# Single-row LSTM as a 2x2 Strassen product, with new tile counts and a planner that reserves result tiles

## The chip, the cores and the metric

The kernel runs on one core of one Trainium2 chip. The metric is device time in microseconds (us), from runs of the whole kernel. The engines are TensorE (PE, matrix products), VectorE (DVE), ScalarE (ACT), GpSimd (POOL) and SyncE (SP, whose queue issues nearly all the DMAs). PEld is the part of TensorE that loads a stationary 128x128 tile.

## The reference

Four layers work on x of 128 batches, 64 rows, 256 features, in float32. Each layer is `x = layernorm(x + f(x))`.

- Layer 0: three graph convolutions with widths 512, 1024 and 256.
- Layer 1: projection on the eigenvectors of a graph Laplacian, two dense layers, and back.
- Layer 2: two graph convolutions with a ReLU give h, and then LSTMs are run over windows of p rows of h, for p = 1, 2, 3, 4 in turn; the last hidden state of each window replaces the last row of that window.
- Layer 3: attention over the 64 rows, masked by the graph.

The part that the change touches is the LSTM with p = 1, where every window is a single row, so that there is no recurrence:

```python
g = x_t @ Wih.T + h @ Whh.T + bias            # h = 0
i, f, gg, o = jnp.split(g, 4, axis=-1)
c = sigmoid(f) * c + sigmoid(i) * tanh(gg)    # c = 0
h = sigmoid(o) * tanh(c)
```

With p = 1 only the gates i, g and o are needed: 768 of the 1024 columns of the weights.

## The kernel before, in words

The 8192 rows are 64 tiles of 128 rows; a *group* is four tiles (8 batches, 512 rows). Layer 0 runs first for all 16 groups, with the eigenvectors worked out beside it; then SBUF is handed over to a second phase, which takes layers 1, 2 and 3 of a group in one go. This second phase is what the change touches.

**Units.** A *unit* is two groups (the last four groups are units of one). A unit notes operations in the order layer1, to_lstm and the LSTMs of p = 1, 2, 3 for each of its groups, then p = 4 for the two together (function `four`), then from_lstm and layer3 for each. Three units are under way at a time (`UNITS`), so one near its end, one in its middle and one at its start can fill each other's waits.

**The planner.** No operation of the second phase is issued where it is written. `Plan.note` records it with an estimated cost, what must come before it and the tiles it touches. `Plan.run` then goes through the recorded operations with a simple clock: for each engine it takes those that could start within 0.02 us of the earliest one, and among these the one with the smallest `rank` (the group number, so the oldest group first). What comes out is a fixed order of instructions for each engine. A tile gets a slot when the first operation that touches it is planned; an operation is ready only when a slot is free (`t = max(t, min(s))`, line 178). Units younger than the oldest leave a few slots of each kind to it (`MOST`).

**Tiles.** PSUM has eight slots of one bank (`ps`). In SBUF there are six work tiles of 128x1024 (`w`; each group's h, called hT, lives in one from to_lstm to from_lstm), four half-size work tiles (`v`), six gate tiles (`gates`), four cell tiles (`c`), four of hidden states (`hs`) and three attention tiles (`att`).

**LSTM with p = 1** (`lstm`, called twice at lines 1290 and 1291, 32 windows of 8 batches each, n = 256). For each half h of the hidden features and each gate of i, g, o it runs two products of 128x128 by 128x256 into one PSUM tile, and ScalarE takes the result straight to a gate tile with bias and tanh (the sigmoid is written with a tanh, which is why factors 0.5 and `op0=ALU.add` with 1.0 appear). VectorE then does one `scalar_tensor_tensor` for i and g, ScalarE a tanh, and VectorE a `scalar_tensor_tensor` that writes h back into hT. For a group this is 24 products of 256 columns.

**Halves** (`halves`, line 1439). The second step of p = 2 and the steps of p = 4 of paired groups already use a seven-product scheme: sums of the weights (`add_weights`) and of the moving operands are built on VectorE, seven products take the place of eight, and VectorE puts the results together with additions that read PSUM.

**The weights.** The four `wih` and three `whh` tiles of 1 MB are loaded by SP at the handover (`load`, lines 857 and 1144), in the order wih0, wih1, whh1, wih2, whh2, wih3, whh3. wih0 is that of p = 1. They are laid out as (k p) f -> p k f, with k the half of the 256 input features.

All the operations of the second phase are issued from one line, 156 (`emit`), so that the profile is read by tile names: `ps<-w,wih` is a product of a work tile with wih, `gates<-gates,ps` an addition of a PSUM tile into a gate tile, and so on.

## Time and profile before

| what | value |
|---|---|
| median of 3 runs | 2471.87 us (2471.45 to 2472.79) |
| time of the profiled execution | 2474.36 us |
| span of the profiled execution | 2472.6 us |
| PE busy | 2438.2 us (99%), 15500 products |
| DVE busy | 1618.9 us (65%), 5676 instructions |
| ACT busy | 1072.3 us (43%), 2610 instructions |
| granted TensorE clock | 0.996 |
| from 861 us to 2472 us (second phase): PE, DVE, ACT busy | 1583.25, 962.74, 757.48 us of 1611 |

How to read the lines: a line of a group is "line engine operation out<-in shape xcount | busy us, mean ns of one | idle time of the engine before them and what ended it". A line of the window view gives for a stretch of the span the length, then the busy time of PE, PEld, DVE, ACT and POOL, each with its number of instructions, then the clock, the DMA share and GB/s. Durations of instructions that follow each other closely overlap, so mean times count is more than busy time. One float32 product of the program appears as two MATMUL instructions.

### The profile page before, as it was taken

How to read it: one execution, taken by the hardware profiler on the slowest of the kernel's cores; microseconds unless marked ns; L12 is line 12 of the kernel's file. 1: busy time of each engine (PE TensorE's matmuls, PEld its weight loads, DVE VectorE, ACT ScalarE, POOL GpSimd, SP SyncE). 2: the span in 40 equal slices, each digit the busy share in tenths (PEclk: the TensorE clock that was granted, in tenths of full speed). 3: DMA queues.
4: the chain of work that ended last, by engine and by line, in shares of the span. 5: the costliest groups of instructions: out<-in, count | busy, mean ns of one | idle time of the engine just before them, and what ended most of it. 6: DMA issues, size and time to landing. Idle time of an engine off the chain costs nothing.

```text
span 2472.6 us, 40811 instructions
## 1 busy us (share of the span) xinstructions
PE 2438.2 (99%) x15500; PEld 2162.5 (87%) x15500; DVE 1618.9 (65%) x5676; ACT 1072.3 (43%) x2610; POOL 137.4 (6%) x316
## 2 busy tenths in 40 slices
PE   9999999999999999999999999999999999999997
PEld 7788888878887899989978999999998997988996
DVE  6888787778887274583674476476458468374336
ACT  2343343333333354444434444444444444445555
POOL 0000000000000010010010000000001001010002
PEclk9999999999999999999999999999999999999999
DMA  6000000000000110010000001001001000000000
GB/s 225 9 1 18 10 9 10 9 10 9 10 1 1 64 56 1 1 35 1 1 18 18 1 1 35 1 1 35 1 1 35 1 1 18 1 10 1 1 1 27
DMA packets 27973, 42.69 MB, mean 17 GB/s; under 512 B 2945, under 2 KB 22145, under 8 KB 27777
## 3 DMA queue, kind: packets, MB, share of 16 engines
q1 hardware_dynamic: 27424, 39.81, 4.6%
q8 instruction: 122, 2.00, 0.3%
q14 instruction: 75, 0.61, 0.1%
q10 hardware_dynamic: 352, 0.28, 0.0%
HBM read 26.45 MB, written 13.63 MB: 16 GB/s over the span
## 4 chain that ended last, share of the span: by engine, by line
PE 93%; DVE 5%; POOL 1%; DMA 1%; ACT 0%; issue 0%; SPq 0%; ACTq 0%; POOLq 0%; DVEq 0%
PE ps L156 61%; PE ps L940 31%; DVE X L156 1%; DVE D L52 1%; DVE st L156 1%; PE pc L296 1%; DMA XA<-in_x_dram 1%; DVE gates L156 0%; POOL rs L156 0%; DVE tw L52 0%; DVE w L156 0%; ACT gates L156 0%; DVE h L52 0%; DVE u L52 0%; DVE mv L156 0%
## 5 line engine op out<-in xcount | busy, mean ns | idle before, releaser
L156 PE MATMUL ps<-w,wih 128*128 128x168 f32 (+2 forms) x4144 | 753.7, 315 | 0.9 <-DVE gates L156 0.9
L156 PEld LDWEIGHTS ps<-w,wih 128*128 128x128 f32 x4144 | 647.6, 191 | 38.1 <-issue 6.9
L156 ACT ACTIVATE gates<-ps,cbi 128x168 f32<-128x168 f32 (+2 forms) x832 | 342.8, 418 | 368.5 <-PE ps L156 360.3
L156 PE MATMUL ps<-hs,whh 128*128 128x168 f32 (+1 forms) x1952 | 344.8, 291 | 0.0
L156 PEld LDWEIGHTS ps<-hs,whh 128*128 128x128 f32 x1952 | 289.2, 191 | 1.7 <-issue 1.4
L156 PE MATMUL ps<-w,sums 128*128 128x128 f32 x1776 | 237.1, 275 | 0.0
L156 DVE SCALAR_TENSOR_TENSOR gates<-gates 128x256 f32<-128x256 f32 (+2 forms) x220 | 84.0, 382 | 222.8 <-ACT gates L156 222.2
L940 PE MATMUL ps<-aw,h 128*128 128x256 f32 x1024 | 227.2, 379 | 0.0
L156 PEld LDWEIGHTS ps<-w,sums 128*128 128x128 f32 x1776 | 217.5, 192 | 0.6 <-issue 0.5
L940 PEld LDWEIGHTS ps<-aw,h 128*128 128x128 f32 x1024 | 192.9, 190 | 25.9 <-ACT h L949 0.5
L156 ACT ACTIVATE gates<-gates,cbi 128x256 f32<-128x256 f32 x272 | 116.4, 497 | 206.6 <-DVE gates L156 206.5
L949 ACT ACTIVATE h<-h 128x512 f32<-128x512 f32 x128 | 80.5, 630 | 196.6 <-DVE h L52 196.5
L156 DVE TENSOR_TENSOR gates<-gates,ps 128x256 f32<-128x256 f32 x340 | 128.7, 417 | 21.3 <-PE ps L156 15.9
L940 PE MATMUL ps<-ss,tw 128*128 128x256 f32 x512 | 117.9, 380 | 0.0
L940 PE MATMUL ps<-ss,aw 128*128 128x256 f32 x512 | 117.3, 379 | 0.0
L940 PE MATMUL ps<-m,aw 128*128 128x256 f32 x512 | 117.1, 380 | 0.0
L156 DVE SCALAR_TENSOR_TENSOR c<-gates,c 128x256 f32<-128x256 f32 (+2 forms) x156 | 57.2, 367 | 88.6 <-ACT gates L156 88.2
L940 PE MATMUL ps<-aw,m 128*128 128x512 f32 x256 | 114.8, 594 | 0.1
L940 PEld LDWEIGHTS ps<-ss,aw 128*128 128x128 f32 x512 | 96.6, 190 | 12.8
L940 PEld LDWEIGHTS ps<-ss,tw 128*128 128x128 f32 x512 | 96.3, 190 | 12.9 <-issue 0.2
L156 DVE TENSOR_TENSOR gates<-v,ps 128x256 f32<-128x256 f32 x136 | 55.5, 417 | 79.5 <-ACT v L156 47.7
L940 PEld LDWEIGHTS ps<-m,aw 128*128 128x128 f32 x512 | 95.6, 190 | 12.6 <-issue 0.5
(314 smaller groups left out, 3743.0 us busy)
## 6 DMA issues: line engine op xcount, KB each, us to landing
out_dram<-X SPq DMA_DIRECT2D x64, 128.0 KB, 1.7
rest<-XA SPq DMA_DIRECT2D x10, 512.0 KB, 2.6
X<-rest SPq DMA_DIRECT2D x10, 512.0 KB, 3.2
XA<-in_x_dram SPq DMA_DIRECT2D x18, 256.0 KB, 6.2
wih<-in_c_ih_dram SPq DMA_DIRECT2D x4, 1024.0 KB, 7.4
aw<-in_a_w_dram SPq DMA_DIRECT2D x3, 1024.0 KB, 10.8
X<-in_x_dram SPq DMA_DIRECT2D x12, 256.0 KB, 5.9
whh<-in_c_hh_dram SPq DMA_DIRECT2D x3, 1024.0 KB, 9.3
```

The costliest lines, as they stand in the source:

```text
L52: return getattr(self.engine, name)(out, *args, **kw)
L156: getattr(e, name)(*[real(x) for x in args], **{k: real(v) for k, v in kw.items()})
L296: PE.matmul(out, lhsT, rhs, start=True, stop=True)
L940: PE.matmul(out, lhsT, rhs, start=start, stop=stop)
L949: S.activation(dst, src, AF.Relu)
```

## The change: what it does

Seven things change together.

1. The two calls of `lstm` with p = 1 are replaced by one call of a new function `single`. It splits the 768 gate columns in two halves m of three 128-column tiles r, the 256 input features in two halves, and the 512 columns of hT in two halves of 32 windows, and works out the 2x2 block product by seven products instead of eight, for each r: 21 products of 128x128 by 128x256 for a group. Sums of the moving operand (T1 to T4) and of the results are made by VectorE.
2. `add_single` makes the weight sums for it once (three new 128x384 tiles, and a fourth that overwrites a block of wih0).
3. wih0 is loaded without the f columns and in a new order, by eight DMAs instead of one.
4. A product now also claims the tiles of SBUF that its result will go to (`also`): it is planned only when a gate tile, and in `halves` and `single` the half-size work tile, is free. Gate tiles that belong together (two, or three in `single`) are claimed together (`tiles`, `along`).
5. Slots: work tiles 6 to 7, gates 6 to 5, att 3 to 2, c 4 to 3.
6. The rank of operations of all engines but PE is the group number plus a third of the time from which the operation is ready. PE keeps the old rank.
7. `unit` calls `add_single` before the other weight sums.

```diff
@@ -92,6 +92,8 @@
         self.tag, self.shape, self.real, self.slot = tag, list(shape), real, None
         self.left, self.until, self.past = 0, 0.0, []
+        self.along = []
     def part(self):
         free = self.shape[1:]
         return Part(self, np.arange(int(np.prod(free))).reshape(free), (0, self.shape[0]), [])
@@ -121,12 +123,23 @@
     def tile(self, tag, shape, real=None):
         return Tile(tag, shape, real).part()
-    def note(self, engine, calls, cost, ready=0.0):
+    def tiles(self, n, tag, shape):
+        parts = [self.tile(tag, shape) for _ in range(n)]
+        for x in parts:
+            x.tile.along = [y.tile for y in parts if y is not x]
+        return parts
+    def note(self, engine, calls, cost, ready=0.0, also=()):
         op = Op()
         op.unit = self.unit
         op.engine, op.calls, op.cost, op.group, op.rank = engine, calls, cost, self.group, len(self.ops)
         op.before, op.after, op.tiles, op.ready, op.start = set(), [], [], ready, None
+        for x in also:
+            op.tiles.append(x.tile)
+            x.tile.left += 1
         for name, args, kw in () if callable(calls) else calls:
             for i, x in enumerate(list(args) + list(kw.values())):
                 if not isinstance(x, Part):
@@ -163,7 +176,9 @@
         def rank(op):
             if op.engine == "PE" and not todo and len(left) <= LASTS:
                 return -left[op.group]
-            return op.group or 99
+            if op.engine == "PE":
+                return op.group or 99
+            return (op.group or 99) + op.ready / 3
         def candidates(guard):
             oldest = min([u for u in going if u] or [0])
@@ -175,7 +190,7 @@
                     for tile in op.tiles:
                         if tile.real is None and tile.slot is None:
                             s = self.slots[tile.tag]
-                            t = max(t, min(s))
+                            t = max(t, sorted(s)[len(tile.along)])
                             if (guard and op.unit != oldest and
                                     sum(x < 1e9 for x in s) <= self.MOST.get(tile.tag, 1) - held.get((oldest, tile.tag), 0)):
@@ -201,7 +216,7 @@
                         able[op.engine].append(op)
             t, op = (candidates(True) if todo or len(left) > LASTS else None) or candidates(False)
             e = op.engine
-            for tile in op.tiles:
+            for tile in [x for tile in op.tiles for x in [tile] + tile.along]:
                 if tile.real is None:
                     s = self.slots[tile.tag]
                     tile.slot, tile.unit = s.index(min(s)), op.unit
@@ -739,10 +754,10 @@
 EPS = 1e-5
 UNITS = 3
 ENDING = (14, 15)
-WIDE = 6
-GATES = 6
-ATT = 3
-CELLS = 4
+WIDE = 7
+GATES = 5
+ATT = 2
+CELLS = 3
 OUTS = 4
 LASTS = 3
 SINGLE = 4
@@ -1141,7 +1156,16 @@
     psb = ctx.enter_context(tc.tile_pool(name="psb", bufs=1, space=bass.MemoryType.PSUM, reuse_waits="tile"))
     wih, whh = [], []
     for i in range(4):
-        wih.append(load(wb, f"wih{i}", c_ih[i], "(k p) f -> p k f", [P, 2, 1024], p=P))
+        if i:
+            wih.append(load(wb, f"wih{i}", c_ih[i], "(k p) f -> p k f", [P, 2, 1024], p=P))
+        else:
+            wih.append(wb.tile([P, 2, 2, 3, P], F32, name="wih0"))
+            w = c_ih[0].rearrange("(k p) f -> p k f", p=P)
+            for m, r, n, f in ((0, 0, 2, 0), (1, 0, 2, 512), (0, 2, 1, 768), (1, 2, 1, 896)):
+                for k in range(2):
+                    nc.sync.dma_start(wih[0][:, k, m, r:r + n, :].rearrange("p r n -> p (r n)"), w[:, k, f:f + n * P])
         whh.append(load(wb, f"whh{i}", c_hh[i], "(k p) f -> p k f", [P, 2, 1024], p=P) if i else None)
     att = []
     for i in range(ATT):
@@ -1189,15 +1213,26 @@
             V.tensor_sub(S3, a11, a21, ready=ready)
             ways[p].append([a11, a12, a22, S1, S2, S3, S4])
-    def products(calls):
+    def add_single():
+        s = plan.tile("sums", [P, 3, 3, P], wb.tile([P, 3, 3, P], F32, name="sums1"))
+        w = plan.tile("sums", [P, 2, 2, 3, P], wih[0])
+        a11, a12, a21, a22 = (w[:, k, m] for m in range(2) for k in range(2))
+        V.tensor_add(s[:, 0], a21, a22, ready=12.0)
+        V.tensor_sub(s[:, 1], s[:, 0], a11, ready=12.0)
+        V.tensor_sub(s[:, 2], a12, s[:, 1], ready=12.0)
+        V.tensor_sub(a21, a11, a21, ready=12.0)
+        ways[1] = [a11, a12, a22, s[:, 0], s[:, 1], a21, s[:, 2]]
+    def products(calls, also=()):
         size = lambda x: x.at.size if isinstance(x, Part) else int(np.prod(x.shape[1:]))
         cost = sum(max(0.001673 * size(c[2]) + 0.003, 0.223) for c in calls)
-        plan.note("PE", [("matmul", (o, l, r), {"start": a, "stop": z}) for o, l, r, a, z in calls], cost)
-
-    def run(out, pairs, first=True, last=True):
+        plan.note("PE", [("matmul", (o, l, r), {"start": a, "stop": z}) for o, l, r, a, z in calls], cost, also=also)
+    def run(out, pairs, first=True, last=True, also=()):
         n = len(pairs)
-        products([(out, l, r, first and i == 0, last and i == n - 1) for i, (l, r) in enumerate(pairs)])
+        products([(out, l, r, first and i == 0, last and i == n - 1) for i, (l, r) in enumerate(pairs)], also)
     def turns(pairs):
         plan.note("PE", [("transpose", (out, in_, ident), {}) for out, in_ in pairs], 0.109 * len(pairs))
@@ -1287,7 +1322,8 @@
             V.scalar_tensor_tensor(as3(h, 4), rs_row.unsqueeze(1).to_broadcast([P, 4, P]), cb1[:, c:c + 1], p,
                                    op0=ALU.mult, op1=ALU.add, cost=0.666)
             S.activation(hT[:, c, :, :].rearrange("p n b -> p b n"), as3(h, 8), AF.Relu, scale=2.0, cost=0.933)
-        for p, first, nw in ((1, 0, 32), (1, 32, 32), (2, 0, 32), (3, 0, 21)):
+        single(hT)
+        for p, first, nw in ((2, 0, 32), (3, 0, 21)):
             lstm(hT, p, first, nw)
         return hT
@@ -1393,8 +1429,8 @@
                        lambda h, w: hT[:, h, 32 * w + 1:32 * w + 32:2, :])
                 return
             gate = []
-            for h in range(2):
-                G = plan.tile("gates", [P, 1024])[:, :len(names) * n].rearrange("p (q n) -> p q n", n=n)
+            for G in plan.tiles(2, "gates", [P, 1024]):
+                G = G[:, :len(names) * n].rearrange("p (q n) -> p q n", n=n)
                 gate.append({q: G[:, i] for i, q in enumerate(names)})
             if p > 1 and not t and not only:
                 c = plan.tile("c", [P, 512])[:, :2 * n].rearrange("p (h n) -> p h n", h=2)
@@ -1409,10 +1445,10 @@
                     outs = [(wh[:, k, m], hs[:, k, :]) for k in range(2)] if t else []
                     if t and h == 0 and q in names[:2]:
-                        run(pp, ins, last=False)
+                        run(pp, ins, last=False, also=[gate[h][q]])
                         run(pp, outs, first=False)
                     else:
-                        run(pp, ins + outs)
+                        run(pp, ins + outs, also=[gate[h][q]])
                     S.activation(gate[h][q], pp, AF.Tanh, bias=bias[:, j:j + 1], scale=0.5 if q == "g" else 0.25)
                     if q == "g":
                         to = gate[h]["g"] if t or p == 1 else c[:, h, :]
@@ -1442,7 +1478,7 @@
         bias = cbi[:, p - 1, :]
-        G = [plan.tile("gates", [P, 1024]).rearrange("p (w m q n) -> p w m q n", w=2, m=2, q=2) for _ in range(2)]
+        G = [x.rearrange("p (w m q n) -> p w m q n", w=2, m=2, q=2) for x in plan.tiles(2, "gates", [P, 1024])]
         both = work().rearrange("p (s i n) -> p s i n", s=2, i=4)
         def eights(v):
@@ -1466,7 +1502,7 @@
                 bank = ps4((P, 2, 2, P))
                 for at, i in enumerate(which):
                     for q in range(2):
-                        run(bank[:, at, q, :], [(ways[p][s][weight[i]][:, q, h, :], moving[i][s]) for s in range(2)])
+                        run(bank[:, at, q, :], [(ways[p][s][weight[i]][:, q, h, :], moving[i][s]) for s in range(2)], also=[a, u1])
                 return bank[:, 0], bank[:, 1]
             p1, p2 = two(0, 1)
@@ -1499,6 +1535,53 @@
                     V.scalar_tensor_tensor(rows(h, w), eights(G[h][:, w, 1, 1, :]), 1.0, eights(G[h][:, w, 0, 0, :]),
                                            op0=ALU.add, op1=ALU.mult)
+    def single(hT):
+        bias = cbi[:, 0, :]
+        x = [[hT[:, k, 32 * w:32 * w + 32, :] for w in range(2)] for k in range(2)]
+        T = work().rearrange("p (i n) -> p i n", i=4)
+        T1, T2, T3, T4 = (T[:, i].rearrange("p (w b) -> p w b", b=8) for i in range(4))
+        V.tensor_sub(T1, x[0][1], x[0][0])
+        V.tensor_sub(T2, x[1][1], T1)
+        V.tensor_sub(T3, x[1][1], x[0][1])
+        V.tensor_sub(T4, x[1][0], T2)
+        moving = (x[0][0], x[1][0], x[1][1], T4, T1, T2, T3)
+        weight = (0, 1, 6, 2, 3, 4, 5)
+        G = [x.rearrange("p (w m n) -> p w m n", w=2, m=2) for x in plan.tiles(3, "gates", [P, 1024])]
+        for r in range(3):
+            u1 = work2()[:, :256]
+            a, b, c12, d = (G[r][:, w, m] for w in range(2) for m in range(2))
+            def two(*which):
+                bank = ps4((P, 2, 256))
+                for at, i in enumerate(which):
+                    run(bank[:, at], [(ways[1][weight[i]][:, r, :], moving[i])], also=[a, u1])
+                return bank[:, 0], bank[:, 1]
+            p1, p2 = two(0, 1)
+            S.copy(u1, p1)
+            V.tensor_add(a, u1, p2)
+            p6, p7 = two(5, 6)
+            V.tensor_add(c12, u1, p6)
+            V.tensor_add(b, c12, p7)
+            p5, p3 = two(4, 2)
+            V.tensor_add(d, b, p5)
+            V.tensor_add(c12, c12, p5)
+            V.tensor_add(c12, c12, p3)
+            p4, _ = two(3)
+            V.tensor_add(b, b, p4)
+            for m, name in ((0, "io"[r // 2]), (1, "go"[r // 2])):
+                j = 2 * "ifgo".index(name) + (r if r < 2 else m)
+                S.activation(G[r][:, :, m, :], G[r][:, :, m, :], AF.Tanh, bias=bias[:, j:j + 1],
+                             scale=0.5 if name == "g" else 0.25)
+            if r < 2:
+                i, g = G[r][:, :, 0, :], G[r][:, :, 1, :]
+                V.scalar_tensor_tensor(g, i, 1.0, g, op0=ALU.add, op1=ALU.mult)
+                S.activation(i, g, AF.Tanh, scale=0.5)
+        for h in range(2):
+            V.scalar_tensor_tensor(hT[:, h, :, :].rearrange("p (w a) b -> p w (a b)", w=2), G[2][:, :, h, :], 1.0,
+                                   G[h][:, :, 0, :], op0=ALU.add, op1=ALU.mult)
     def four(hTs):
         n = 128
@@ -1518,6 +1601,7 @@
     def unit(groups):
         if groups[0] == 0:
+            add_single()
             add_weights(2, 30.0)
             add_weights(4, 60.0)
         xs, hTs = [], []
```

## The prediction

> **What bounds the kernel now.** I read the page's first part and its chain first, then the costliest groups by form, then the second phase in stretches of 20 to 50 us, then single stretches in order of time. The page:
>
> ```profile
> PE 2438.2 (99%) x15500; PEld 2162.5 (87%) x15500; DVE 1618.9 (65%) x5676; ACT 1072.3 (43%) x2610; POOL 137.4 (6%) x316
> PE 93%; DVE 5%; POOL 1%; DMA 1%; ACT 0%; issue 0%; SPq 0%; ACTq 0%; POOLq 0%; DVEq 0%
> ```
>
> TensorE is busy for 99% of the span and carries 93% of the chain. I checked that this is work and not modelled ends: counting each MATMUL of the second phase at its spacing in the timeline gives 1594 us, and the phase's products run from 861 us to about 2450 us, 1589 us: full, within the rounding of the spacings. So products taken away are time taken away, as long as something else is there for TensorE to do.
>
> The products that the change touches, in the timeline, and the VectorE kinds of which more will come (groups by form):
>
> ```profile
> 891.37 10.53 PE L156 MATMUL ps<-w,wih 128*128 128x256 f32 x48
> 901.73 1.89 PE L156 MATMUL ps<-cw,w 128*128 128x256 f32 x8
> ...
> L156 DVE TENSOR_TENSOR gates<-gates,ps 128x256 f32<-128x256 f32 x340 | 128.7, 417 | 21.3 <-PE ps L156 15.9
> L156 DVE SCALAR_TENSOR_TENSOR gates<-gates 128x256 f32<-128x256 f32 x132 | 55.7, 422 | 93.0 <-ACT gates L156 92.5
> ```
>
> 48 MATMULs (one group's p = 1) take 901.73 - 891.37 = 10.36 us, 0.2158 us each. VectorE's 0.417 us is a duration; at 1076.43 us two such instructions lie in 0.75 us, so the second starts 0.33 us after the first. A saturated VectorE pays 0.33, an idle one 0.42.
>
> The second phase in windows (length; PE, PEld, DVE, ACT, POOL busy):
>
> ```profile
> 1140.00:1160.00 20.00, 20.00 (x118) 17.03 (x117) 6.75 (x17) 11.13 (x28) 0.00 (x0) 1.00 0.00 1
> 1541.00:1561.00 20.00, 20.00 (x123) 17.34 (x122) 6.48 (x17) 10.51 (x27) 0.00 (x0) 1.00 0.00 1
> ...
> 1061.00:1101.00 40.00, 40.00 (x266) 32.15 (x266) 37.25 (x115) 21.85 (x44) 9.82 (x20) 1.00 0.11 37
> 1461.00:1501.00 40.00, 39.66 (x288) 33.08 (x288) 37.92 (x117) 20.25 (x45) 7.53 (x16) 1.00 0.03 8
> ...
> 1250.00:1300.00 50.00, 46.18 (x316) 35.69 (x314) 41.19 (x120) 18.44 (x36) 7.87 (x18) 0.97 0.07 22
> 2035.00:2085.00 50.00, 46.36 (x307) 36.73 (x306) 43.85 (x131) 24.30 (x48) 9.70 (x20) 1.00 0.05 17
> ```
>
> This is what decides. About every 200 us one unit ends (from_lstm, layer3) while the next begins, and VectorE is then 93 to 95% busy for 40 us. By the timeline, the first group's p = 1 products of the middle unit lie in five of these stretches (around 1061, 1461, 1661, 1850 and 2061 us). They are TensorE's cover there: 10.36 us of products for eight VectorE instructions. At 1250 us, where no p = 1 products lie, TensorE stands idle for 3.8 us. The other groups' p = 1 (around 1140, 1305, 1363, 1541, 1741, 1941 us and the last units) lie where VectorE is a third busy.
>
> **What the skill says.** The Trainium skill, "Perfetto Trace Analysis", section Identifying the Most-Contended Engine, warns that matmul busy time is a poor measure and asks for the weight-load share: PEld is 87% here, and 95% or more only in stretches of 128-column products; hence my count by spacing. The same page, section Optimizing Scalar/DVE Operations, puts VectorE's own overhead at about 60 ns on SBUF and 125 ns on PSUM, with latency about twice that; the trace has 0.33 us between and 0.42 us alone at 256 elements, 0.60 and 0.68 at 512. "VectorE: DVE Perf Modes", section The perf-mode tier table, says that a float32 tensor_tensor has no faster mode, so the additions can't be had more cheaply; 0.417 us here for SBUF and PSUM operands alike agrees.
>
> **The change, part by part.**
>
> *TensorE.* 24 products become 21 for a group: 6 MATMULs fewer x 0.2158 = 1.295 us; x 16 groups = **20.7 us off**. The weight load (0.190 us) stays under the 0.2158 of a MATMUL, so no load comes to the front.
>
> *VectorE.* For each group: +4 sums of the moving operand and +21 additions, 25 x 0.417; -8 scalar_tensor_tensor of 256, x 0.422; +4 of 512 at 0.681 (the row X<-X,wide_b_b 128x512). 10.43 - 3.38 + 2.72 = +9.8 us by durations, 25 x 0.33 - 8 x 0.33 + 4 x 0.60 = +8.0 us when saturated. The whole is +128 to +157 us on 1618.9. Beside 9.06 us of products, single wants about 10.7 us of VectorE: it no longer covers anything, it wants cover. Where VectorE is a third busy (11 of 16 groups) the other units' products hide that: 20 us with 7 busy have room for 8. In the five full stretches the room is 40 - 37.25 = 2.75 us, so up to 8.0 - 2.75 = 5.3 us each comes out as TensorE waiting, **0 to +26.5 us**. What can lower it: p = 3 needs 21.6 us of TensorE and some 6 of VectorE for a group, and layer1 and to_lstm of the youngest unit can come earlier, which a seventh work tile allows (six hold the hT of three units with none left over). Both are only as good as the planner's order. I take 1.8 us for each stretch, **+9 us**: a third of the whole bound, since layer3's own operations keep their place at the head and one or two products of p = 2 or p = 3 can be drawn forward.
>
> *ScalarE.* 12 activations of 256 (0.474) and 4 (0.410) become 6 and 2 of 512 (0.63 to 0.71) and 3 copies (0.365): 7.3 to about 6.6 us. ScalarE is under 60% everywhere; nothing on the path.
>
> *Weight sums, once.* 4 x about 0.55 us (384 elements, between 0.417 and 0.684) at 12 us of plan time, near 873 us; VectorE has 15 of 20 us busy there and TensorE has six groups' layer1 to do. Nothing, or 2.2 us if it falls on the first chain.
>
> *Loads.* SP issued wih0 and wih1 at 845.24 us in 0.90 us, then stood until 859.05 us. Eight issues at 0.45 are 3.6 us; wih1 goes out by about 849.5 and what is behind it waits for 859 anyway. Landing took 5.1 to 12.4 us; the sums need wih0 at 873. Nothing; without that gap 3.2 us, once.
>
> *Claiming tiles, five gates.* A halves or p = 3 step holds two gate tiles for its products (12.5 or 9.1 us) and a tail of some 4 us; two such chains hide each other's tails with four tiles, and single's three with one chain's two fill five. What is lost is a third chain, and TensorE can no longer run ahead of ScalarE's gates. Bounds: -4 us (fewer PSUM tiles stand full waiting for a gate, which may be part of the 3.8 us stalls) to +1 us for each group, +16. I take +1 in all, as the waits name gate tiles as what a product or its weight load waits for only for 3.8 us in the whole run (PE 0.9, PEld 2.9).
>
> *Rank with age.* It lets a younger group's additions go ahead once they are some 6 us late (two groups x 3 us), freeing PSUM tiles. -5 to +3; I take -1. *att, c.* Two layer3 at once need two; the end, where four half-size layer3 follow one another, may lose 0 to +2. I take 0.
>
> Sum: -20.7 + 9 + 1 - 1 = -11.7 us on a span of 2472.6 and a profiled time of 2474.36; that execution stands 2.5 us above the median, so I apply the difference to the median: 2471.87 - 11.7 = **2460 us**.
>
> **The rivals.**
>
> *A. The whole saving, or more* (2447 to 2453). The planner puts single where VectorE is light; stalls at 1250 and 2035 us shrink too. For it: 65% of VectorE leaves 850 us. Against: oldest first gives the middle unit its turn just when the oldest ends.
>
> *B. VectorE becomes the bound in the full stretches* (2478, slower). Five stretches x 5.3 - 20.7 = +6. It decides slower from (20.7 + 4.9) / 5 = 5.1 us a stretch. For it: 93% already, and the cover gone; gate tiles held by a starved single make it longer, up to 2486. Against: only five of sixteen.
>
> *C. The saving is eaten by claims* (2467 to 2476). If each single and each next step waits 0.8 to 1.6 us more for its gate tiles, 16 x 1.3 = 20.7 is gone. For it: three at once out of five. Against: p = 1 work is filler, and a filler that waits costs only if there is no other.
>
> *D. The products don't get as cheap as counted*, because each is now alone in its sum instead of one of a pair. Attention's lone products (ps<-w,v 128x256, 1093.37 to 1095.14 us) are eight in 1.77 us, 0.221 each, elsewhere up to 0.229: at most 42 x 0.013 x 16 = 9 us given back, 2469.
>
> **How the numbers follow.** Likeliest case 0.47 (2454 to 2466), A 0.18, B 0.22, C and D 0.13. Range for eight in ten: 2446 to 2484, from A's good end to most of B. This kernel's runs lie within 0.06%, and 0.2% (4.9 us) is about what a measurement can tell from no change. Faster: the likeliest case and A, 0.65. Same: most of C, 0.12. Slower: B and a little of C, 0.23.
>
> **What would show it.** `ps<-w,wih` 128x256 falls from 1152 to 768, a new `ps<-w,sums` 128x256 has 288, PE has 15404 products, those of 256 spaced 0.216; gates<-gates,ps goes to 580 and gates<-v,ps to 232; DVE busy 1745 to 1776. PE's idle time between 861 and 2450 us grows by about 9 us, in stretches with VectorE above 93%, ended by DVE. If it grows by over 20, B or C is right, told apart by whether VectorE was full. I am wrong if the end of the span (2450 to 2472.6) moves, or if the first products of p = 1 wait for wih0.

## The result, and the profile after

The kernel after takes 2467.31 us (median of 20 runs, 2465.84 to 2469.49) against 2472.67 us for the kernel before in the same comparison: ratio 0.9979, 95% interval 0.9972 to 0.9985. That is 5.4 us faster, less than half of the 11.7 us that I forecast. The profiled execution took 2467.51 us, with a span of 2465.7 us.

The page of the kernel after, its engines and its chain:

```profile
PE 2423.0 (98%) x15404; PEld 2144.7 (87%) x15404; DVE 1743.3 (71%) x6016; ACT 1060.6 (43%) x2530; POOL 135.4 (5%) x315
PE 85%; DVE 11%; ACT 2%; issue 1%; DMA 0%; POOL 0%; SPq 0%; ACTq 0%; DVEq 0%
```

The MATMULs fell by 96, as counted, and VectorE rose by 124 us, just under the 128 to 157 that I had counted. The chain shows the price: TensorE's share fell from 93 to 85%, VectorE's rose from 5 to 11%. The groups by form of the kernel after have the counts that I gave:

```profile
L169 DVE TENSOR_TENSOR gates<-gates,ps 128x256 f32<-128x256 f32 x580 | 220.2, 416 | 23.5 <-PE ps L169 15.9
L169 PE MATMUL ps<-w,wih 128*128 128x256 f32 x768 | 193.5, 382 | 1.0 <-DVE w L169 0.9
L169 DVE TENSOR_TENSOR gates<-v,ps 128x256 f32<-128x256 f32 x232 | 94.0, 416 | 51.2 <-ACT v L169 26.9 <-PE ps L169 23.8
L169 PE MATMUL ps<-w,sums 128*128 128x256 f32 x288 | 78.8, 380 | 0.3 <-DVE w L169 0.3
```

The second phase as one window, from 861 us to the end of the last product; length, then PE, PEld, DVE, ACT and POOL busy. First the kernel before, then the kernel after:

```profile
861.00:2459.30 1598.30, 1583.24 (x11441) 1463.05 (x11439) 956.48 (x2798) 754.21 (x1834) 96.56 (x201) 1.00 0.04 12
```

```profile
861.00:2452.70 1591.70, 1567.60 (x11338) 1444.61 (x11336) 1080.96 (x3137) 742.93 (x1754) 95.39 (x201) 1.00 0.04 12
```

TensorE's idle time (length less PE) went from 15.1 to 24.1 us. That is the +9 us of the forecast, but it is not all: TensorE's busy time fell by only 15.6 us where the work fell by 20.7. A part of these 5 us are MATMULs at half clock, shown below; the rest lies in gaps too short to show, because the modelled end of a MATMUL (0.38 us) reaches over the start of the next (0.216 us later). Where the idle time lies, in windows of the kernel after:

```profile
1121.00:1161.00 40.00, 40.00 (x271) 38.54 (x270) 22.74 (x66) 20.74 (x52) 1.01 (x2) 1.00 0.00 1
...
1250.00:1270.00 20.00, 17.51 (x102) 13.20 (x101) 19.83 (x62) 10.07 (x20) 3.90 (x8) 1.00 0.00 1
1835.00:1865.00 30.00, 27.06 (x195) 22.50 (x194) 27.84 (x83) 14.07 (x28) 3.90 (x8) 1.00 0.01 2
2040.00:2060.00 20.00, 16.30 (x85) 13.44 (x84) 18.79 (x60) 8.74 (x20) 1.96 (x6) 0.85 0.00 1
```

In the quiet stretch nothing is lost. Where a unit ends, VectorE is busy 93 to 99% and TensorE loses 2.5 to 3.7 us. One of these places in order of time, kernel after:

```profile
1847.66 0.75 DVE L169 TENSOR_TENSOR gates<-gates,ps 128x256 f32<-128x256 f32 x2
1848.33 0.74 DVE L169 TENSOR_TENSOR gates<-v,ps 128x256 f32<-128x256 f32 x2
...
1852.71 0.70 DVE L169 TENSOR_SCALAR X<-X,mv,rs 128x256 f32<-128x256 f32 x2
...
1853.14 0.76 PE L169 MATMUL ps<-ident,X 128*128 128x128 f32 x4 [1.70 <-DVE X L169]
```

The additions of a younger group's single (1847.66, 1848.33) share VectorE with the ending unit's norm; the transposes of layer3 wait 1.70 us for that norm. Four additions take 1.33 us of VectorE here.

A stop can cost more than its own length. The longest stop of the kernel after, in order of time, and the granted clock just behind it:

```profile
2043.40 0.59 PE L169 MATMUL ps<-w,sums 128*128 128x256 f32 x2
2043.83 0.59 PE L169 MATMUL ps<-w,wih 128*128 128x256 f32 x2
...
2054.81 1.51 PE L169 MATMUL ps<-ident,X 128*128 128x128 f32 x6 [3.29 <-DVE X L169]
2056.11 1.06 PE L169 MATMUL ps<-w,wih 128*128 128x256 f32 x2
2056.97 0.64 PE L169 MATMUL ps<-ident,X 128*128 128x128 f32 x2
```

```profile
2055.00:2058.00 3.00, 3.00 (x12) 2.62 (x12) 2.53 (x7) 1.08 (x2) 0.00 (x0) 0.50 0.00 0
```

Two MATMULs of 256 columns take 0.43 us ahead of the stop (2043.40 to 2043.83) and 0.86 us behind it (2056.11 to 2056.97), where the granted clock is 0.50. Not every stop is followed by this: the window from 1835 to 1865 us, with the stop of 1.70 us, has a clock of 1.00 throughout. By the clock records of the two traces, TensorE runs at half clock for 10.2 us of the second phase before and 13.7 us after, up to the last product. At the spacing above that cost about 5.1 and 6.8 us (an estimate: half of the time at half clock).

### The profile page after: what moved, and what is told of

Same layout as the page of the kernel before. It is cut to its first block, busy times and chain, and to the rows that moved or that the text cites. A ratio compares the mean times of both kernels' runs of the same rounds, so it can differ in the third digit from the quotient of the medians.

```text
span 2465.7 us, 40936 instructions
## 1 busy us (share of the span) xinstructions
PE 2423.0 (98%) x15404; PEld 2144.7 (87%) x15404; DVE 1743.3 (71%) x6016; ACT 1060.6 (43%) x2530; POOL 135.4 (5%) x315
## 4 chain that ended last, share of the span: by engine, by line
PE 85%; DVE 11%; ACT 2%; issue 1%; DMA 0%; POOL 0%; SPq 0%; ACTq 0%; DVEq 0%
PE ps L169 52%; PE ps L955 31%; DVE gates L169 3%; DVE X L169 2%; ACT gates L169 2%; DVE w L169 1%; DVE st L169 1%; DVE D L52 1%; PE pc L311 1%; DMA XA<-in_x_dram 0%; DVE v L169 0%; DVE c L169 0%; DVE tw L52 0%; POOL rs L169 0%; ACT w L169 0%
## 5 line engine op out<-in xcount | busy, mean ns | idle before, releaser
L169 PE MATMUL ps<-w,wih 128*128 128x128 f32 (+2 forms) x3760 | 687.9, 308 | 1.0 <-DVE w L169 0.9
L169 PEld LDWEIGHTS ps<-w,wih 128*128 128x128 f32 x3760 | 574.9, 191 | 25.5 <-issue 3.8
L169 ACT ACTIVATE gates<-ps,cbi 128x168 f32<-128x168 f32 (+2 forms) x640 | 253.1, 399 | 308.6 <-PE ps L169 300.3
L169 PE MATMUL ps<-w,sums 128*128 128x128 f32 (+1 forms) x2064 | 314.1, 290 | 0.3 <-DVE w L169 0.3
L169 ACT ACTIVATE gates<-gates,cbi 128x256 f32<-128x256 f32 (+1 forms) x368 | 182.8, 555 | 234.1 <-DVE gates L169 233.9
L169 PEld LDWEIGHTS ps<-w,sums 128*128 128x128 f32 x2064 | 269.6, 192 | 9.7 <-issue 2.2
L169 DVE TENSOR_TENSOR gates<-gates,ps 128x256 f32<-128x256 f32 x580 | 220.2, 416 | 23.5 <-PE ps L169 15.9
L169 DVE SCALAR_TENSOR_TENSOR gates<-gates 128x168 f32<-128x168 f32 (+3 forms) x188 | 79.1, 421 | 150.4 <-ACT gates L169 149.3
L169 DVE TENSOR_TENSOR gates<-v,ps 128x256 f32<-128x256 f32 x232 | 94.0, 416 | 51.2 <-ACT v L169 26.9
L169 ACT ACTIVATE gates<-c 128x168 f32<-128x168 f32 (+2 forms) x252 | 90.4, 360 | 42.7 <-DVE c L169 41.7
```

The lines of the kernel that those rows point to most:

```text
L169: getattr(e, name)(*[real(x) for x in args], **{k: real(v) for k, v in kw.items()})
```

## The experiments

Times are medians. A difference without another name is to the kernel before in the same comparison (2472.26 to 2473.47 us); one to the kernel after is between the two medians, and steps between two other kernels are differences of their differences to before. Two kinds of run must be kept apart. In four of them the list of instructions on each engine is that of the kernel named, but for some that are cut short or left out. In the others the planner makes a new order, so that a step of a few microseconds holds for that order.

### The same order: is a product time, and is VectorE a bound?

**Three products less, nothing added.** In `lstm` of the kernel before, after the product is noted and planned at its full cost:

```diff
                         run(pp, ins + outs)
+                        if p == 1 and h and not first:
+                            name, args, kw = plan.ops[-1].calls[0]
+                            plan.ops[-1].calls = [(name, args, {"start": True, "stop": True})]
```

> The kernel before, in its own order of instructions, with three of the 24 products of p = 1 of each group simply not issued (those of the second 128 input features for the second half of the gates, in the first call; the gates there come out incomplete). No VectorE work is added. Theory 1 (a product taken from TensorE is time, and what the change failed to give was eaten by VectorE): -18 to -21 us on before, nearly the whole 96 x 0.2158 = 20.7. Theory 2 (TensorE's 99% hides a second limit, the fixed order and the chains of waits): -3 to -10 us, as little as the change itself gave.

Measured: 2456.86 us, ratio 0.9937 (0.9923 to 0.9950), 15.6 us faster. Three quarters of the 20.7 us arrive, between the two theories and nearer to theory 1. A quarter is lost though no work was added, so even before the change the product was not always what ended last.

**VectorE lighter in the kernel after.** An operation marked `lite` is planned at full cost and issued on 2 columns:

```diff
+        if op.lite:
+            full = real
+            real = lambda x: full(x)[:, :2] if isinstance(x, Part) and x.at.size > 2 else full(x)
...
             V.tensor_add(c12, c12, p5)
+            plan.ops[-1].lite = True
             V.tensor_add(c12, c12, p3)
+            plan.ops[-1].lite = True
...
             V.tensor_add(b, b, p4)
+            plan.ops[-1].lite = True
```

and the same mark on the `tensor_scalar` of `norm`.

> The kernel after, in its own order, with three in-place additions of each r in single and the twelve scalings of the layer norms of each group cut to 2 columns (the rest of their columns is left as it is): about 9 x 0.25 + 12 x 0.25 = 5.3 us of VectorE less for each group, 84 us in all; products and ScalarE are the same. Theory 1 (VectorE full in the stretches where a unit ends): 6 to 12 us faster than after, the half or more of the 13 us that TensorE lost. Theory 2 (the order itself and the claims make TensorE wait): within 2 us of after.

Measured: 2452.70 us, ratio 0.9920 (0.9906 to 0.9933); 14.6 us under the kernel after. The window of this kernel:

```profile
861.00:2438.10 1577.10, 1560.37 (x11337) 1441.49 (x11335) 1030.04 (x3137) 742.60 (x1754) 92.78 (x201) 1.00 0.04 12
```

VectorE's busy time is 50.9 us lower than after (not the 84 of my count: on 2 columns a scaling still took 0.283 us instead of 0.407, an addition 0.150 instead of 0.416), with products and ScalarE's work unchanged, and TensorE's idle time is down from 24.1 to 16.7 us. The gain is more than theory 1 had. VectorE does bound this kernel in places: each microsecond taken from it gave 0.29 us.

**The norms alone in the kernel before.** The same mark on `norm` only.

> The kernel before, in its own order, with the same twelve scalings of the layer norms of each group cut to 2 columns: 48 us of VectorE less. The pair to the run on the kernel after. Theory 1: VectorE bounds only short places before, so 2 to 5 us faster than before, clearly less than the light kernel after gains. Theory 2: the same gain in both, or none in both.

Measured: 2467.26 us, ratio 0.9980 (0.9971 to 0.9988), 5.2 us faster for 20.0 us of VectorE, 0.26 us for each, hardly less than in the kernel after. So VectorE bounded part of the kernel before too.

**Single's in-place additions alone in the kernel after.** The marks in `single` without that in `norm`.

> The kernel after, in its own order, with only the three in-place additions of each r in single cut to 2 columns (9 x 0.25 = 2.25 us of VectorE less for each group, 36 us in all, of some 130 that single adds); the norms are whole. It splits the 14.6 us that the lighter kernel after gained. Theory 1 (single's own work in the full stretches): 5 to 9 us faster than after. If the norms gave it all: within 2 us of after.

Measured: 2459.41 us, ratio 0.9947 (0.9935 to 0.9960), 7.9 us under the kernel after for 31.7 us of VectorE, 0.25 us for each. The norms' part of the earlier gain is then 14.6 - 7.9 = 6.7 us, if the two parts add, close to the 5.2 of the kernel before. Single's own additions are paid for at about a quarter of their time, on the whole; single adds 124 us.

### New orders: which part gave the gain?

**Everything but single.** The kernel after with p = 1 by `lstm`, wih0 whole, no `add_single`.

```diff
-        single(hT)
-        for p, first, nw in ((2, 0, 32), (3, 0, 21)):
+        for p, first, nw in ((1, 0, 32), (1, 32, 32), (2, 0, 32), (3, 0, 21)):
             lstm(hT, p, first, nw)
```

> The kernel after with p = 1 given back to lstm (24 products, no sums, wih0 loaded whole); claims, slot counts 7, 5, 2, 3 and the rank with age stay. My prediction: claims +1, rank -1, slots 0: within 3 us of before. Theory 1: the same, -2 to +2. Theory 2 (five gates and claims cost what is missing): 5 to 10 us slower than before.

Measured: 2465.74 us, ratio 0.9974 (0.9964 to 0.9984), 6.7 us faster. Neither forecast: without single the rest of the change gives as much as the whole. Single adds +1.3 us to it, which the intervals do not tell from nothing.

**The seventh work tile alone.** The kernel before with two numbers traded for one:

```diff
-WIDE = 6
+WIDE = 7
-ATT = 3
-CELLS = 4
+ATT = 2
+CELLS = 3
```

> The kernel before with seven work tiles instead of six, paid for by att 3 to 2 and c 4 to 3; six gates, the old rank, no claims, 24 products. The run with the surroundings alone was 6.7 us faster than before. Theory S (the seventh work tile is what the surroundings gave, because with six the hT of three units leave none for intermediate results): 5 to 12 us faster than before. Theory R (the rank with age gave it): within 3 us of before.

Measured: 2457.65 us, ratio 0.9940 (0.9927 to 0.9954), 15.8 us faster: more than theory S had, and nearly three times the whole change, with every product of the kernel before. Its windows:

```profile
861.00:2442.30 1581.30, 1576.67 (x11439) 1458.64 (x11437) 956.11 (x2798) 756.14 (x1834) 97.80 (x201) 1.00 0.04 12
...
1250.00:1300.00 50.00, 49.55 (x324) 39.48 (x323) 43.90 (x131) 25.47 (x53) 10.24 (x20) 1.00 0.13 43
```

TensorE's idle time is 4.6 us instead of 15.1, and it is never at half clock, where the kernel before spent 10.2 us: 10.5 us less idle and about 5.1 us less lost to the clock make up nearly the whole difference. From 1250 to 1300 us, where the kernel before lost 3.8 us, this one loses 0.45. VectorE's work is the same and as dense there. The edit leaves only the work tile as the reason, since the other two counts were cut. I read it as cover: with a free work tile, products of another unit can be under way, which the windows fit but do not show one by one. The Trainium skill, "Perfetto Trace Analysis", section Optimization Strategy, says that the same gap coming back on an engine that should be full can mean that there is not enough SBUF or PSUM for the next tile. With the seventh tile the stalls at 1250 and 2035 us, of 3.8 and 3.6 us in the windows of the prediction, are all but gone. They did not come back in every period, though: the ends of units at 1061 and 1461 us in the same windows lost nothing and 0.3 us.

**Five gates as well, no claims.** All four slot counts of the change in the kernel before.

> The kernel before with the four slot counts of the change (seven work tiles, five gates, att 2, c 3), without claims and with the old rank. If the five gates cost the 4.5 us: about 2462. If the claims do: about 2458, as with seven work tiles and six gates.

Measured: 2457.27 us, ratio 0.9938 (0.9923 to 0.9953). Five gate tiles cost nothing.

**Claims and slots.** The kernel after without single and with the old rank.

> The kernel after without single (24 products by lstm) and with the old rank: claims and slots 7, 5, 2, 3 alone are left of the change. Theory S: as fast as with seven work tiles alone, within 4 us, so that the claims cost little. Theory R: back at the time of before, within 3 us.

Measured: 2462.16 us, ratio 0.9955 (0.9943 to 0.9968), 11.3 us faster, 4.5 us behind seven work tiles alone, just outside theory S's 4: the claims cost 4.1 us of the 15.4. Adding the rank with age gives the run without single, 6.7 us faster, so the rank cost 4.6 us there.

**The old rank with single.** In the kernel after:

```diff
-            if op.engine == "PE":
-                return op.group or 99
-            return (op.group or 99) + op.ready / 3
+            return op.group or 99
```

> The kernel after with the old rank on VectorE and ScalarE (oldest group first); single, claims and slots stay. My prediction: the rank is worth 1 us. If VectorE is full, its order decides who starves: then the additions of single of the younger unit come late and hold PSUM and gate tiles, and this is 5 to 20 us slower than after. If VectorE is not what bounds, within 3 us of after.

Measured: 2495.55 us, ratio 1.0093 (1.0080 to 1.0107), 28 us over the kernel after, more than I had expected. Its second phase, and a window of it:

```profile
861.00:2485.90 1624.90, 1587.00 (x11340) 1453.05 (x11338) 1085.13 (x3138) 742.70 (x1754) 96.92 (x201) 0.98 0.03 12
1400.00:1600.00 200.00, 190.35 (x1343) 172.20 (x1342) 133.26 (x382) 84.95 (x197) 9.81 (x20) 0.97 0.04 12
```

TensorE idles 9.7 us of 200 with VectorE two thirds busy: it is the order on VectorE, not its load alone. In the whole phase TensorE idles 37.9 us, 13.8 more than in the kernel after, and by the clock record it spends 54.6 us at half clock against 13.7. By half of that difference, about 20 of the 33 us between the two profiled executions (2500.95 and 2467.51 us) went to the lower clock. The runs of this kernel agree: 2500.95 us at a mean granted clock of 0.987, 2492.49 us at 0.990. With single the age is worth 28 us; without, it costs 4.6.

**Six work tiles with single.** The kernel after with `WIDE = 6`.

> The kernel after with six work tiles instead of seven. single takes a work tile for its sums T1 to T4 while the hT of up to three units lie in the others. If the seventh tile's worth is the same with and without single: about 16 us slower than after, 2483. If single needs it (the younger units can't begin while sums and hT fill the six): 30 to 90 us slower than after.

Measured: 2561.15 us, ratio 1.0357 (1.0341 to 1.0372), 94 us over the kernel after. Two windows of it:

```profile
1000.00:1200.00 200.00, 178.35 (x1204) 160.88 (x1203) 122.92 (x349) 76.56 (x181) 8.31 (x18) 0.93 0.03 11
...
1400.00:1600.00 200.00, 178.50 (x1252) 162.95 (x1250) 127.47 (x367) 78.26 (x181) 9.74 (x20) 0.94 0.04 12
```

TensorE stands still 11% of the time in these windows and no engine is full. Its clock record has 88.8 us at half clock, so that by the same estimate the clock accounts for some 38 of the 94 us. single takes one work tile for its sums, and so the seventh tile is first of all what it needs to be planned well; on its own it would have been a gain.

### Where single pays

**Second groups only**, and its mirror. `add_single` keeps its fourth sum in a tile of its own, and wih0 is read in its new layout by `lstm`. Of the last four groups, which are units of one, every other one counts as a second group:

```diff
-        single(hT)
+        if (plan.group - 1) % 2:
+            single(hT)
+        else:
+            for first in (0, 32):
+                lstm(hT, 1, first, 32)
```

> The kernel after in which only the odd groups (the second of each pair) use single; the even ones have the 24 products of lstm. In the kernel before the second groups' p = 1 lay where VectorE was a third busy. Half of the products' saving is left (8 x 1.295 = 10.4 us) and half of the VectorE work (4 us a group). Place theory (only the first groups' single meets a full VectorE): 5 to 10 us faster than the surroundings alone (2465.7), so 2456 to 2461, and faster than after. Load theory (any VectorE work added costs in proportion): half way between after and the surroundings alone, 2466 to 2467.

> The mirror: only the even groups (the first of each pair) use single. Place theory: slower than after, 2470 to 2485, since these lie where a unit ends and VectorE is full. Load theory: 2466 to 2467, the same as with the second groups.

Measured: second groups 2457.53 us, ratio 0.9940 (0.9928 to 0.9953); first groups 2477.73 us, ratio 1.0020 (1.0012 to 1.0028). Both have the same products, the same VectorE work (1018.59 and 1021.53 us busy in the phase) and the same settings, and they lie 20 us apart. Against the run without single, second groups gain 8.0 us of the possible 10.4, and first groups lose 12.2 us. Windows around single's products, second groups and then first groups:

```profile
1147.00:1162.00 15.00, 15.00 (x91) 13.71 (x90) 12.33 (x32) 8.28 (x16) 0.00 (x0) 1.00 0.01 1
1536.00:1551.00 15.00, 15.00 (x90) 13.71 (x90) 11.68 (x31) 8.45 (x16) 0.00 (x0) 1.00 0.00 1
1346.00:1361.00 15.00, 14.62 (x81) 12.68 (x80) 15.00 (x44) 7.41 (x12) 2.28 (x4) 1.00 0.00 0
```

```profile
1480.00:1488.00 8.00, 4.22 (x30) 3.59 (x28) 8.00 (x27) 0.37 (x1) 1.93 (x4) 1.00 0.20 67
1853.00:1881.00 28.00, 25.07 (x157) 19.70 (x156) 26.02 (x78) 12.39 (x25) 3.91 (x8) 0.94 0.00 1
```

In the first two windows of second groups VectorE has room and TensorE never stops. In these two of first groups VectorE is at 93 to 100% and TensorE stops for 3 to 4 us. The place decides, and the load theory (2466 to 2467 for both) falls. But a full VectorE alone is not what costs the time: in the third window it is busy throughout, and TensorE loses 0.38 us. What differs is what waits for it. The transposes of X in layer3, with their waits, in the run without single, with second groups, with first groups, and in the kernel after:

```profile
L169 PE MATMUL ps<-ident,X 128*128 128x128 f32 x128 | 19.8, 282 | 1.8 <-ACT X L169 1.8
L169 PE MATMUL ps<-ident,X 128*128 128x128 f32 x128 | 18.3, 274 | 0.8 <-ACT X L169 0.8
L169 PE MATMUL ps<-ident,X 128*128 128x128 f32 x128 | 20.9, 289 | 10.7 <-DVE X L169 9.3 <-ACT X L169 1.3
L169 PE MATMUL ps<-ident,X 128*128 128x128 f32 x128 | 22.2, 296 | 10.0 <-DVE X L169 8.2 <-ACT X L169 1.8
```

Where first groups use single, these transposes wait 8 to 9 us for VectorE to finish the norm of the ending unit; in the other two runs they show no wait for VectorE. The stop at 1484 us in the run with first groups is of the same kind: there ScalarE waits 4.77 us for the attention's softmax on VectorE, and three of single's sums (1485.70, 1486.03 and 1487.76 us) lie between its steps.

**Second groups, weaker age.** As above with `op.ready / 12`.

> Only the odd groups use single, and the age counts a twelfth instead of a third in the rank of VectorE and ScalarE, so that an older unit keeps its place for 24 us instead of 6. If the rank with age costs the older units time (4 to 5 us between the two runs without single) and single in the light places is a gain: 2449 to 2456, faster than both kernels and than seven work tiles alone. If age is needed wherever single is used: slower than with a third.

Measured: 2451.18 us, ratio 0.9914 (0.9901 to 0.9928), 21.1 us faster than before and 16 us faster than the kernel after, with nothing left out. Its window shows 7.2 us of TensorE's idle time:

```profile
861.00:2436.50 1575.50, 1568.27 (x11387) 1452.82 (x11386) 1020.61 (x2972) 746.33 (x1794) 96.64 (x203) 1.00 0.04 12
```

**Second groups, old rank.**

> Only the odd groups use single, with the old rank (oldest group first, no age). If a starved single is what made the old rank 28 us slower than after, it is far less where VectorE is light: 2456 to 2466. If the age is needed as such: over 2475.

Measured: 2462.59 us, ratio 0.9961 (0.9947 to 0.9975). The old rank costs 5 to 11 us here against the two ages, not 28. That fits a starved single of the first groups as what needed the age; the waits of that single were not followed one by one.

**Sums on GpSimd.** T1 to T4 of `single` in the kernel after:

```diff
-        V.tensor_sub(T1, x[0][1], x[0][0])
+        K.tensor_sub(T1, x[0][1], x[0][0], cost=0.7)
```

and the other three likewise, with K the notes for GpSimd.

> The kernel after with the four sums T1 to T4 of single on GpSimd, which is 5% busy, planned at 0.7 us each; the result is complete. VectorE has 4 x 0.33 = 1.3 us less for each group, 21 us in all. Theory 1 (VectorE bounds): 3 to 10 us faster than after. Theory 2, and also if GpSimd is slow at 128x256: same or slower.

Measured: 2460.92 us, ratio 0.9952 (0.9940 to 0.9965), 6.4 us under the kernel after, as theory 1 has it. Half of the 64 sums (the other half, w<-w,w, has a mean of 784 ns), then one place in this run where sums run beside VectorE, and the same VectorE instruction in the kernel after:

```profile
L169 POOL TENSOR_TENSOR w<-w 128x256 f32<-128x256 f32 x32 | 24.2, 759 | 515.3 <-ACT w L169 323.4 <-DVE gates L169 97.4 <-PE ps L169 94.6
...
1152.69 0.73 POOL L169 TENSOR_TENSOR w<-w,w 128x256 f32<-128x256 f32 x1 [8.94 <-ACT gates L169]
1152.70 1.60 DVE L169 SCALAR_TENSOR_TENSOR c<-gates 128x128 f32<-128x128 f32 x2 [1.32 <-ACT gates L169]
...
L169 DVE SCALAR_TENSOR_TENSOR c<-gates 128x128 f32<-128x128 f32 x32 | 9.2, 288 | 8.5 <-ACT gates L169 8.5
```

GpSimd needs 0.76 us for a sum that spaces VectorE by 0.33, and is idle enough for it to be a gain. But VectorE was relieved by less than I had counted: its busy time fell by 11.4 us, not 21. Beside sums on GpSimd, two VectorE instructions that read SBUF alone took 1.60 us where one takes 0.29. Not all were slowed so: ten of gates<-gates 128x168 took 0.337 us beside a sum instead of 0.333, and thirteen additions with an operand in PSUM kept their 0.416 us. Since the order is new too, how much of the 6.4 us is VectorE's relief and how much the order stays open.

## Why the prediction was right or wrong

The time lay in the range and the sign was right, but the size was not, and two of its terms were far off in opposite directions. That it came out faster at all is luck: the seventh work tile, which I had put at nothing, outweighed what I had missed in the other terms. The runs give this ladder (microseconds against the kernel before; each line adds one part):

| with | difference | step | my step |
|---|---|---|---|
| seven work tiles, att 2, c 3 | -15.8 | -15.8 | 0 |
| five gates | -15.4 | +0.4 | 0 |
| claims | -11.3 | +4.1 | +1 |
| rank with age | -6.7 | +4.6 | -1 |
| single (products and VectorE) | -5.4 | +1.3 | -11.7 |

*The products.* Right in count, spacing and in that each is time: 96 MATMULs at 0.2158 us. The lone products are not wider (in the timeline of the kernel after, pairs at 890.99, 891.42 and 891.85 us are 0.43 apart), so rival D falls. But "products taken away are time taken away" held for 15.6 of 20.7 us where nothing else changed. The count that it rested on was wrong: with the median spacings of that trace (0.112, 0.143, 0.216 and 0.429 us for 128, 168, 256 and 512 columns) the products come to about 1575 us, not 1594, and the last one ends at 2459 us, not 2450. So the 1598 us of the phase were not full: about 23 us were free, 15.1 of them idle and 5.1 lost to the clock. I had also seen that five of sixteen groups' products lie where VectorE is 93% busy, and charged only the added VectorE work there, not a part of the saving that a full VectorE can't let through; that would fit the lost quarter, but no run shows where it was lost.

*VectorE*, one of the two steps that failed. I took +9 us, a third of the bound, on the ground that other products could be drawn forward. Against the run without single the cost is 20.7 + 1.3 = 22 us, near my upper bound of 26.5; some 5 of it are the quarter of the saving that was lost without any VectorE work too, if that holds in this order. The mechanism (first groups lose where a unit ends, second groups don't) is shown by the mirror pair, with 12.2 lost and 8.0 gained; the size was wrong. What could not be drawn forward is the norm of the ending unit, for which the transposes of X wait 8.2 us in the kernel after, and I left out that MATMULs behind a stop can run at half clock. TensorE's idle time did grow by 9.0 us, but over an order that has 10.6 us without single and 4.6 us without claims and age, so that agreement is no support for the term.

*Slots*, the other step that failed, and the larger. I put the seventh work tile at nothing by itself, and counted it only as something that might lower VectorE's term, though I had noted that six tiles hold the hT of three units with none left over, and that TensorE stood idle at 1250 and 2035 us. It is worth 15.8 us, as it removes 10.5 of the 15.1 us of TensorE's idle time before and all of the 10.2 us at half clock: the largest miss of all. Five gates at nothing was right.

*Claims and rank.* Within my bounds (claims up to +16, rank -5 to +3) for the claims at +4.1; the rank at +4.6 without single is outside, and with single it is worth 28 us the other way. I priced each alone; the rank has no price of its own, it depends on whether starving work stands behind it. Both are single orders, and other orders may give other numbers.

*The rest.* SP's eight issues went out from 844.44 us in 3.94 us, wih1 followed at 848.42, and whh1 stood until 858.25 us (859.05 before); the tail after the last attention product is unchanged; ScalarE came out 12 us lower. All at nothing, as said.

*The rivals.* The time is at the edge of C, but not for its reason: five gates cost nothing and claims 4 us. B's mechanism was there (TensorE waits for VectorE where a unit ends) and came to 22 us against its 26.5; what kept the kernel from B's time is the seventh tile. Neither the likeliest case nor a rival had two large terms that cancel.

## What to carry to other kernels

Trading products for VectorE work pays where nothing that TensorE needs next stands behind that work: the same code gained 8.0 us in eight groups and lost 12.2 us in the other eight, where the norm of an ending unit had to share VectorE with it. So look at the stretch in which the products serve as cover before taking their count for a saving. When a change brings its own buffers, price the buffers alone first: here one more work tile was worth 15.8 us without a new product scheme, and the best kernel (2451.18 us) is the new scheme in half of the groups with that tile and a weaker age. A stall where one unit ends and the next begins can be a question about buffers before it is one about engines. And count what lies behind a stop, not only the stop: here the half clock that followed some of them cost from nothing (seven tiles alone) to some 44 us (six tiles with single), by the estimate above.

## What the runs showed of the hardware

- An addition that reads PSUM is spaced like one on SBUF alone: two gates<-gates,ps of 128x256 in 0.75 us, 0.33 us from start to start, as the pair of scalar_tensor_tensor on SBUF in the prediction.
- TensorE's busy time is not its work: with MATMULs recorded as 0.38 us and spaced by 0.216, gaps of up to 0.16 us do not show as idle. It fell by 15.6 us where 20.7 us of work had gone; about 1.7 of the difference is half clock, by the estimate above.
- After a stop of 3.29 us the granted clock was 0.50 and MATMULs of 256 columns were 0.43 us apart instead of 0.216. How long a stop has to be for this is not shown.
- GpSimd takes 0.76 us for a float32 subtraction of 128x256 in SBUF; VectorE 0.42 alone and 0.33 in a row. Beside such subtractions, two VectorE instructions of 128x128 on SBUF took 1.60 us (0.29 for one otherwise); others on SBUF, and additions with an operand in PSUM, kept their time.
- Cut from 256 to 2 columns, an in-place addition went from 0.416 to 0.150 us, but the scaling of a norm (tensor_scalar with two columns of scalars) only from 0.407 to 0.283.
